# Sort's place stage held until the messages are done, the count stage's bank with its low digits outermost, and sort's operands loaded a group ahead

## The chip, the core and the metric

The kernel runs on one core of a Trainium2 chip. The metric is the device time of one execution in microseconds (us). Its engines are TensorE (PE, with its weight loads shown apart as PEld), VectorE (DVE), ScalarE (ACT), GpSimd (POOL) and SyncE (SP). In this kernel POOL does nothing but issue indirect DMAs (gathers and scatters by a list of rows, one for each 128 rows) after a few set-up instructions, and SP issues all other DMAs. Each engine runs its own instructions strictly in the order in which the program was built; semaphores tie the engines together.

## The reference, cut to what matters

Three branches are computed from the same normed nodes `xn` (3125 x 256) and added:

```python
def gnn(nodes, edges, senders, receivers, W_message, ...):
    msg_in = jnp.concatenate([nodes[senders], edges], axis=-1)         # 103125 x 320
    agg = jax.ops.segment_sum(msg_in @ W_message, receivers, 3125)
    h = layer_norm(relu(agg) + nodes, ...)
    return layer_norm(nodes + relu_mlp_skip(h, ...), ...)

def mix(x, ...):                                                       # 4 layers
    for i in range(4):
        x = x + linear_attn(layernorm(x), ...)                         # softmax over nodes for the keys
        x = x + gelu(layernorm(x) @ W1[i] + b1[i]) @ W2[i] + b2[i]

def ffn(x, ..., edge_index):                                           # 65536 edges, 4 experts
    h = x @ W_gat
    e = leaky_relu(a_src[src] + a_dst[dst]);  alpha = softmax of e over the edges of one dst
    agg = segment_sum(h[src] * alpha, dst);  w = top-2 gates of layernorm(agg)
    return sum over experts of gate * (gelu(x @ W1 + b1) @ W2 + b2)

xn = layernorm(x)
x = x + gnn(xn, ...) + mix(xn, ...)
x = x + ffn(layernorm(x), ...)
```

The `gnn` edges come sorted by receiver; the 65536 edges of `ffn` don't, so the kernel sorts them by `dst` itself.

## The kernel before, in words

Nodes lie in 25 tiles of 128 rows. Four kinds of work run side by side until about 1930 us; the last 520 us are the edges' softmax and the experts.

*Messages.* The 103125 edges are laid out as 128 partitions by 806 columns, so that each partition holds a run of edges in order of receiver. For each column, line 515 gathers one row of `xn` per partition (POOL), an SP load brings the edge features (line 494), and line 527 on DVE adds the column before it where the receiver stays the same. Columns come in chunks of 8 with three buffers (`m_run`); a finished chunk is stored to `run_d` (line 532). When all are summed, `message_nodes` closes the stage: `carries` (line 475) adds what crosses partitions, `fetch` gathers the sums of two node tiles at a time (line 595), and `pair` is the branch's MLP on them, a generator cut into `piece`s.

*The mixer.* Four layers over seven chunks of four tiles (`norm1`, `keys`, `context`, `combined`, `attend`, `ff_up`, `ff_down`), on PE, ACT and DVE. Line 1118 is the first product of each layer's `combined`.

*The sort* of the 65536 edges by `dst`, in 64 groups (`GROUPS`) of 8 columns of 128 edges (`GC`). A `dst` is split into a high digit (128 bins) and a low one (`LO` = 32). `count_group` makes one-hots of both digits on DVE (lines 695 and 701), multiplies them on PE (line 716) into a bank of PSUM laid out as column by low digit, evicts it on ACT into `cnts` (line 718), a 16-bit tile laid out as low digit by column, stores that to `counts_d` (line 719), and adds it to the table of all counts on PE one group later (line 723). `cnts` has two buffers. After the counts, `starts` makes the first place of each bin, `edge_ranges` the range of each node, and `ends_tile` (25 times) finds where each node's messages end. Then `place_group`, 64 times: SP loads the group's high digits as rows copied to all partitions (`hr`, 256 KB, line 756), DVE compares them with the partition's number (line 758) and makes the low one-hots again (`low_hots`, line 759), a scan (line 761) turns the stored counts into running ones, PE counts equal high digits among a column's edges (line 775), ACT turns that into "earlier" (line 776), and in the call after it PE and DVE look up each edge's place (lines 781 to 791). Every fourth call finishes 32 columns of `place`, and `clock["placed"]` says how many are ready. `send` (line 802) scatters one column of edges to its places (line 805, POOL).

*The edges' softmax and the experts.* Once all 512 columns are sent, `sorted_edges` loads the sorted list back and line 1294 gathers table rows by it (325 indirect DMAs), beside the expert MLPs on PE.

What sets the order is a planner that runs while the program is built. `clock["now"]` is a planned time; each step of the mixer calls `pace(us)`, which moves it on, runs one message `piece` if there is any, and adds every column that is due at `FIRST + COLUMN * (columns + 1)`, that is one per 1.27 planned us. When the last column is in, it sends up to 24 columns (`EARLY`), runs the jobs up to `ends_done`, and calls `message_nodes`; from then on columns are sent at the same spacing, as far as they are placed. The sort's steps stand in `jobs`; `beside(us)` runs as many as their planned costs allow (1.0 for a count group, 4.0 for a place group), but while messages are under way only as long as more than `held[0]` jobs are left. `held[0]` starts at `GROUPS - 12` and falls by 14 with each layer, so the place stage is spread over all four layers.

Of the kernel before, what the change touches and what calls it, by code (L numbers as in the profile page):

```python
# [8 lines left out]
F32 = mybir.dt.float32  # L9
BF16 = mybir.dt.bfloat16  # L10
I32 = mybir.dt.int32
F16 = mybir.dt.float16
# [6 lines left out]
P = 128  # L19
# [10 lines left out]
TM = -(-E // P)  # L30
# [5 lines left out]
DEPTH = 4  # L36
# [4 lines left out]
TE = E2 // P  # L41
NEXP = 4
GC = 8
GROUPS = TE // GC
SRC = 4096
LO = 32
# [13 lines left out]
def kernel(ctx: ExitStack, tc: tile.TileContext, a: dict, out: bass.AP):  # L60
    nc = tc.nc
# [174 lines left out]
    ps = pg.tile([P, DM], F32, name="ps_g")  # L236
# [171 lines left out]
        V.tensor_scalar(above, node_n, -1.0, SRC // 2 - 0.5, op0=ALU.mult, op1=ALU.add)  # L408

    def ends_tile(t):  # L410
        buf = so.tile([P, 8 * P], F16, name="ends_buf", tag="hr", bufs=2)
        at_least = buf[:, 6 * P:7 * P]
        V.tensor_scalar(at_least, row0, start_t[:, t:t + 1], None, op0=ALU.is_ge)
        T.matmul(first_ps[:, t:t + 1], at_least, ones_h, start=True, stop=True, skip_group_check=True)
        le, own = buf[:, :P], buf[:, P:2 * P]
        V.tensor_scalar(le, ids, whole_t[:, t:t + 1], None, op0=ALU.is_ge)
        T.matmul(whole_ps[:, t:t + 1], le, ones_h, start=True, stop=True, skip_group_check=True)
        V.scalar_tensor_tensor(own, ids, prev_t[:, t:t + 1], le, op0=ALU.is_ge, op1=ALU.subtract)
        for k, (c0, c1) in enumerate(((0, TM // 2), (TM // 2, TM))):
            ps = pa.tile([P, 512], F32, name="ps_a")  # L420
            T.matmul(ps[:, :c1 - c0], own, dst_h[:, c0:c1], start=True, stop=True)
            hit = buf[:, 2 * P:2 * P + TM // 2]
            S.activation(hit, ps[:, :c1 - c0], AF.Sign, bias=above[:, t:t + 1], accum_out=cnt2n[:, k, t:t + 1])
# [117 lines left out]


    FIRST, COLUMN, PIECE, EARLY = 52.0, 1.27, 0.9, 24
    clock = {"now": 45.0, "columns": 0, "sent": 0}

    pieces = []

# [4 lines left out]

    def pace(us):
        clock["now"] += us
        if pieces:
            piece()
        pinned = True
        while clock["columns"] < TM and FIRST + COLUMN * (clock["columns"] + 1) <= clock["now"]:
            sum_up(clock["columns"], pinned)
            pinned = False  # L560
            clock["columns"] += 1
            if clock["columns"] == TM:
                while clock["sent"] < min(EARLY, clock["placed"]):
                    send(clock["sent"])
                    clock["sent"] += 1
                for _ in range(len(jobs) - N_JOBS + ENDS):
                    jobs.pop(0)[1]()
                msgs.close()
                message_nodes()
        while (clock["columns"] == TM and clock["sent"] < clock["placed"]  # L570
               and FIRST + COLUMN * (TM + clock["sent"]) <= clock["now"]):
            send(clock["sent"])
            clock["sent"] += 1
# [125 lines left out]
    def low_hots(t):  # L699
        o = so.tile([P, GC, LO], F16, name="oh_lo", bufs=3)  # L700
        V.tensor_tensor(o, low_ids.rearrange("p (o l) -> p o l", o=1).to_broadcast([P, GC, LO]),
                        lo[:, t:t + GC].rearrange("p (t o) -> p t o", o=1).to_broadcast([P, GC, LO]), op=ALU.is_equal)
        return o

    counts_d = dram.tile([GROUPS, P, LO * (GC + 1)], F16, name="counts_d")
    counted = []
    cnts = [so.tile([P, LO, GC + 1], F16, name=f"counts{k}") for k in range(2)]
    for o in cnts:
        V.memset(o[:, :, 0], 0.0)

    def count_group(t):
        if t < TE:
            ohh, ohl = one_hot(t, hi, P, "oh_hi", 2), low_hots(t)
            ps = pg.tile([P, GC, LO], F32, name="ps_g")
            for i in range(GC):
                T.matmul(ps[:, i, :], ohh[:, :, i], ohl[:, i, :], start=i == 0, stop=i == GC - 1, skip_group_check=True)
            cnt = cnts[t // GC % 2]
            S.copy(cnt[:, :, 1:].rearrange("p l i -> p i l"), ps)  # L718
            nc.sync.dma_start(counts_d[t // GC, :, :], cnt.rearrange("p l i -> p (l i)"))
            counted.append((t, cnt))  # L720
        if t:
            t, cnt = counted.pop(0)
            T.matmul(table, ident_h, cnt.rearrange("p l i -> p (l i)"), start=t == 0, stop=t + GC == TE, skip_group_check=True)

    def split(x, near, rest):

        V.tensor_copy(near, x)
        V.tensor_tensor(rest[:, :, 0], x, near, op=ALU.subtract)
# [6 lines left out]
    def starts():  # L735
        cnt2 = so.tile([P, LO], F32, name="cnt2", tag="base")
        V.tensor_reduce(cnt2, table.rearrange("p (l i) -> p l i", i=GC + 1), AX.X, ALU.add)
        cum2 = so.tile([P, LO], F32, name="cum2", tag="oh_lo", bufs=3)
        V.tensor_tensor_scan(cum2, ones[:, :LO], cnt2, 0.0, op0=ALU.mult, op1=ALU.add)
        ps = pg.tile([P, LO], F32, name="ps_g")  # L740
        T.matmul(ps[:, :1], before, cum2[:, LO - 1:], start=True, stop=True)
        V.tensor_tensor(cum2, cum2, cnt2, op=ALU.subtract)
        base2 = so.tile([P, 1], F32, name="base2")
        V.tensor_copy(base2, ps[:, :1])
        V.tensor_scalar(cum2, cum2, base2, None, op0=ALU.add)
        nc.sync.dma_start(start_d, cum2)
        V.tensor_scalar(cum2, cum2, half, None, op0=ALU.add)
        places.append(parts(0))
        split(cum2, *places[0])

    def place_group(t):

        late = looks.pop() if looks else None
        if t < TE:
            hr = so.tile([P, GC, P], F16, name="hr", bufs=2)
            nc.sync.dma_start(hr.rearrange("p t e -> p (t e)"), row_h[t // GC:t // GC + 1, :].to_broadcast([P, P * GC]))
            ohT = ohTs[t // GC % 2]
            V.tensor_scalar(ohT[:P - 1], hr[:P - 1], bin_p[:P - 1], 2.0, op0=ALU.is_equal, op1=ALU.mult)
            ohl = low_hots(t)
            near, run_l = places.pop()  # L760
            V.tensor_tensor_scan(run_l.rearrange("p l i -> p (l i)"), goes.rearrange("p l i -> p (l i)"),
                                 run_l.rearrange("p l i -> p (l i)"), 0.0, op0=ALU.mult, op1=ALU.add)
# [15 lines left out]
        if late:  # L778
# [9 lines left out]
                    T.matmul(look[:, i, :], a1, a2, start=False, stop=k == 2, skip_group_check=True)  # L788
            own = so.tile([P, GC, LO], F32, name="own_bin", bufs=1)
            V.scalar_tensor_tensor(own, look, float(E2), ohl, op0=ALU.add, op1=ALU.mult)  # L790
            V.tensor_reduce(number[t // SG % 2][:, t % SG:t % SG + GC], own, AX.X, ALU.add)
            if (t + GC) % SG == 0:
                V.tensor_scalar_mul(number[t // SG % 2], number[t // SG % 2], 0.5)
# [2 lines left out]

    places = []
    looks = []
    SG = 4 * GC
    number = [so.tile([P, SG], F32, name=f"number{i}") for i in range(2)]  # L800

# [12 lines left out]
    ENDS = GROUPS + 1 + 2 + NT + 6  # L814
    jobs.insert(ENDS - 1, (1.0, ends_done))
    N_JOBS = len(jobs)
    held = [GROUPS - 12]
    spare_us = [0.0]

    def beside(us):  # L820
# [332 lines left out]
    def ff_down(l, c):  # L1153
        for i0, ts in enumerate(halves(c)):
# [9 lines left out]
            if l < DEPTH - 1:  # L1164
                for t in ts:
                    stats(xm[:, t, :], mv[:, t, :])
            beside(3.0 if 0 < l < DEPTH - 1 else 12.0)

    waiting = []
    gT = mx.tile([P, FF // P, 512], F32, name="gT")  # L1170
# [8 lines left out]
    for l in range(DEPTH):  # L1179
# [1 line left out]
        if l == 0:  # L1181
            fold(0)
        co = combined(kv, l)
        held[0] = GROUPS - 12 - 14 * l + 9 * (l > 0)
        beside(20.0)
        held[0] = GROUPS - 12 - 14 * l
        if l + 1 < DEPTH:
            att_w[l + 1] = layer_weights(l + 1)
        if l:
# [536 lines left out]
```

## Time and profile before

| | us |
|---|---|
| median of 3 runs (2451.12 to 2457.45) | 2451.38 |
| the profiled execution | 2454.66 |
| its span, first to last instruction | 2452.9 |

| where | from | to |
|---|---|---|
| layer 0 begins (line 1118) | 144 | |
| count groups on PE (line 716) | 145 | 335 |
| place groups on PE (line 775) | 500 | 1786 |
| layers 1, 2, 3 begin (line 1118) | 690, 1072, 1607 | |
| message gathers (line 515) | 34 | 1195 |
| scatters of sorted edges (line 805) | 1197 | 1908 |
| fetches of message sums (line 595) | 1232 | 1580 |
| row gathers of sorted edges (line 1294) | 1932 | 2349 |

The profile is of one execution. A group of instructions has one row: line, engine, operation, output and inputs, count, then busy time in us and the mean of one in ns, then how long the engine stood idle before such instructions and who ended that. "Issue" is time in which the engine waited for nothing that the profile shows. A row of waits reads: who waited, for whom, us in total, how often, and the longest.

### The profile page before, as it was taken

The numbers are of one execution on the slowest core, as the hardware profiler recorded it, in microseconds if no ns is written. First come the engines' busy times: TensorE is split into PE (matmuls) and PEld (weight loads), VectorE is DVE, ScalarE is ACT, GpSimd is POOL, SyncE is SP. The second block draws the span as 40 slices with busy tenths as digits, with TensorE's granted clock in tenths as the row PEclk, the third lists the DMA queues.
The fourth block names the chain that finished last, engine by engine and source line by source line (L and its number), as shares of the span: only waits on it lengthen the run. The fifth ranks groups of instructions, "written<-read, shape, count | busy, mean of one in ns | idle before, by whom it ended". The sixth has DMA issues, their size and how long they took to land. (4 is left out here: it accounts for less than half of the span.)

```text
span 2452.9 us, 32199 instructions
## 1 busy us (share of the span) xinstructions
PE 2048.4 (84%) x10075; PEld 1417.6 (58%) x10075; DVE 1510.4 (62%) x4536; ACT 1171.0 (48%) x2042; POOL 1720.3 (70%) x1740
## 2 busy tenths in 40 slices
PE   3869868686869998869589988989999889999976
PEld 2656645455546766646455666666767555556545
DVE  8886767758786776776534445466542355556536
ACT  5646565344444454445336656566544233333324
POOL 4666667757777777767767777777777777777742
PEclk9978878787889998979889999999999999999988
DMA  8986778878987888888611111222210112121101
GB/s 252 321 258 214 238 219 259 230 201 288 313 283 234 279 256 265 264 266 254 200 38 31 47 40 36 65 69 51 69 39 12 23 29 50 28 48 31 27 14 61
DMA packets 301773, 362.12 MB, mean 148 GB/s; under 512 B 183099, under 2 KB 248740, under 8 KB 288388
## 3 DMA queue, kind: packets, MB, share of 16 engines
q1 hardware_dynamic: 233076, 245.26, 31.6%
q0 software_dynamic: 68512, 114.67, 17.6%
q8 instruction: 82, 1.34, 0.2%
q14 instruction: 103, 0.84, 0.1%
HBM read 203.75 MB, written 160.11 MB: 148 GB/s over the span
## 5 line engine op out<-in xcount | busy, mean ns | idle before, releaser
L515 POOL DMA_INDIRECT m_run<-xn_d,src_i x806 | 814.2, 1010 | 376.3 <-issue 213.9
L805 POOL DMA_INDIRECT by_dst<-pairs,place x512 | 505.7, 988 | 156.1 <-issue 154.0
L527 DVE SCALAR_TENSOR_TENSOR m_run<-m_run,stay 128x320 f32<-128x320 f32 x805 | 439.2, 546 | 85.2 <-DMA m_run<-xn_d,src_i 72.3
L1149 PE MATMUL ps_a<-h,w 128*128 128x512 f32 (+1 forms) x896 | 387.7, 577 | 6.2 <-ACT h L165 6.1
L1294 POOL DMA_INDIRECT rows_c<-tab_d,si x325 | 319.1, 982 | 98.9 <-issue 97.1
L1160 PE MATMUL ps_a<-w,gT 128*128 128x256 f32 x1600 | 365.1, 383 | 0.0
L1160 PEld LDWEIGHTS ps_a<-w,gT 128*128 128x128 f32 x1600 | 303.1, 192 | 50.3 <-issue 7.6
L1149 PEld LDWEIGHTS ps_a<-h,w 128*128 128x128 f32 x896 | 164.7, 202 | 165.2 <-issue 146.0
L1150 ACT ACTIVATE gT<-ps_a,b 128x512 f32<-128x512 f32 (+1 forms) x224 | 140.8, 637 | 131.2 <-PE ps_a L1149 129.8
L124 ACT ACTIVATE hn<-xm,rstd 128x256 f32<-128x256 f32 x225 | 120.8, 594 | 60.3 <-DVE rstd L120 56.3
L776 ACT ACTIVATE earlier<-ps_t,slope 128x512 f16<-128x512 f32 x128 | 93.8, 772 | 115.0 <-PE ps_t L775 112.3
L160 PE MATMUL ps_t<-ident,hn 128*128 128x128 f32 x450 | 82.4, 313 | 48.5 <-ACT hn L124 41.8
L1415 ACT ACTIVATE hf<-ps_a,be 128x512 f32<-128x512 f32 (+1 forms) x112 | 70.3, 641 | 103.8 <-PE ps_a L1411 103.0
L1061 PE MATMUL ps_a<-wq,h 128*128 128x256 f32 x400 | 100.5, 394 | 20.0 <-ACT kT L1041 14.6
L1087 PE MATMUL ps_g<-xm,kr 128*128 128x256 f32 x400 | 108.1, 408 | 9.8 <-ACT kr L1085 9.5
L1029 PE MATMUL ps_a<-h,wk 128*128 128x512 f32 (+1 forms) x224 | 104.8, 604 | 2.7 <-ACT h L165 2.7
L1426 PE MATMUL ps_t<-we2h,hf 128*128 128x256 f32 x400 | 95.9, 392 | 10.8 <-ACT hf L1415 10.8
L160 PEld LDWEIGHTS ps_t<-ident,hn 128*128 128x128 f32 x450 | 56.0, 156 | 82.7 <-ACT hn L124 60.9
L1087 PEld LDWEIGHTS ps_g<-xm,kr 128*128 128x128 f32 x400 | 77.4, 202 | 42.0 <-ACT kr L1085 26.6
L718 ACT CAST counts<-ps_g 128x256 f16<-128x256 f32 x64 | 79.8, 1393 | 45.3 <-DMA counts_d<-counts 22.0
L1138 PE MATMUL ps_a<-co,hT 128*128 128x256 f32 x400 | 99.7, 392 | 0.8 <-DVE co L1129 0.6
L1061 PEld LDWEIGHTS ps_a<-wq,h 128*128 128x128 f32 x400 | 75.4, 195 | 40.8 <-ACT kT L1041 16.7
(441 smaller groups left out, 3812.4 us busy)
## 6 DMA issues: line engine op xcount, KB each, us to landing
run_d<-m_run SPq DMA_DIRECT2D x100, 1280.0 KB
m_run<-in_edge_attr_dram SPq DMA_DIRECT2D x95, 256.0 KB
hr<-row_h SPq DMA_DIRECT2D x64, 256.0 KB
m_run<-xn_d,src_i POOLq DMA_INDIRECT x806
w<-in_L_mix_W_dram SPq DMA_DIRECT2D x8, 1024.0 KB
by_dst<-pairs,place POOLq DMA_INDIRECT x512
rows_c<-tab_d,si POOLq DMA_INDIRECT x325
run_d<-rows_c SPq DMA_DIRECT2D x15, 312.0 KB
```

Of the source, the lines that this page charges most:

```text
L124: S.activation(dst, src, AF.Identity, bias=r[:, 1, i:i + 1], scale=r[:, 0, i:i + 1])
L160: T.transpose(ps[:, i * P:(i + 1) * P], src[:, c * P:(c + 1) * P], ident)
L515: last_gather[0] = G.indirect_dma_start(out=m[:, t, :D], out_offset=None, in_=xn_d, in_offset=bass.IndirectOffsetOnAxis(ap=src_i[:, t0 + t ...
L527: add = V.scalar_tensor_tensor(m[:, t, :], before_m, stay[:, c:c + 1], m[:, t, :], op0=ALU.mult, op1=ALU.add)
L805: i = G.indirect_dma_start(out=by_dst, out_offset=bass.IndirectOffsetOnAxis(ap=place[:, t:t + 1], axis=0), in_=pairs0[:, t:t + 1], in_offs ...
L1029: T.matmul(ps[:, :n], att_w[l]["wk"][:, kc, m * P:(m + 1) * P], h1[:, kc, :n], start=kc == 0, stop=kc == 1)
L1061: T.matmul(ps[:, i, :], h1[:, kc, o + i * P:o + (i + 1) * P], att_w[l]["wq"][:, kc, :], start=kc == 0, stop=kc == 1)
L1087: T.matmul(ps_x[:, m, :], kr[:, m * P:(m + 1) * P], xm[:, t, :], start=i == 0 and m == 0, stop=i == len(c) - 1, skip_group_check=True)
L1149: T.matmul(ps[:, :w], ff_w[l]["w1"][:, kc, f * P:(f + 1) * P], h2[:, kc, :w], start=kc == 0, stop=kc == 1)
L1150: S.activation(gT[:, f, :w], ps[:, :w], AF.Gelu, bias=ff_w[l]["b1"][:, f:f + 1])
L1160: T.matmul(ps[:, i, :], gT[:, f, (2 * i0 + i) * P:(2 * i0 + i + 1) * P], ff_w[l]["w2"][:, f, :], start=False, stop=f == FF // P - 1, skip_ ...
L1294: G.indirect_dma_start(out=rows_c[:, t - COLS[j], :], out_offset=None, in_=tab_d, in_offset=bass.IndirectOffsetOnAxis(ap=si[:, t:t + 1], a ...
```

## The change

- `held[0]` is `GROUPS - 5` throughout: until the last message column is summed the jobs stop with 59 left, which leaves six calls of `place_group` before it. After that `beside` gets 14 planned us, not 3, in the middle layers (and in the last one), once the messages are done.
- When the messages are done, pieces of the message MLP are held back for `COLUMN * (EARLY + 8)` = 41 planned us.
- The count stage's bank is laid out as low digit by column, so a product writes every eighth element of it and the eviction runs along both its sides. `cnts` gets four buffers (the two new ones share the tag of `run`), and a group is added to the table two groups later instead of one.
- The low one-hots of each count group are stored to DRAM (`lows_d`), and the place stage loads them instead of comparing again.
- `hr` and the low one-hots of a place group are loaded two calls ahead (`ahead_of`), the first two groups' in `starts`. `ends_buf` takes the tag `earlier` instead of `hr`.

```diff
--- before.py
+++ after.py
@@ -408,7 +408,7 @@
         V.tensor_scalar(above, node_n, -1.0, SRC // 2 - 0.5, op0=ALU.mult, op1=ALU.add)

     def ends_tile(t):
-        buf = so.tile([P, 8 * P], F16, name="ends_buf", tag="hr", bufs=2)
+        buf = so.tile([P, 8 * P], F16, name="ends_buf", tag="earlier", bufs=2)
         at_least = buf[:, 6 * P:7 * P]
         V.tensor_scalar(at_least, row0, start_t[:, t:t + 1], None, op0=ALU.is_ge)
         T.matmul(first_ps[:, t:t + 1], at_least, ones_h, start=True, stop=True, skip_group_check=True)
@@ -541,7 +541,7 @@


     FIRST, COLUMN, PIECE, EARLY = 52.0, 1.27, 0.9, 24
-    clock = {"now": 45.0, "columns": 0, "sent": 0}
+    clock = {"now": 45.0, "columns": 0, "fetched": 0.0, "sent": 0}

     pieces = []

@@ -552,7 +552,7 @@

     def pace(us):
         clock["now"] += us
-        if pieces:
+        if pieces and clock["now"] >= clock["fetched"]:
             piece()
         pinned = True
         while clock["columns"] < TM and FIRST + COLUMN * (clock["columns"] + 1) <= clock["now"]:
@@ -567,6 +567,7 @@
                     jobs.pop(0)[1]()
                 msgs.close()
                 message_nodes()
+                clock["fetched"] = clock["now"] + COLUMN * (EARLY + 8)
         while (clock["columns"] == TM and clock["sent"] < clock["placed"]
                and FIRST + COLUMN * (TM + clock["sent"]) <= clock["now"]):
             send(clock["sent"])
@@ -705,22 +706,25 @@
     counts_d = dram.tile([GROUPS, P, LO * (GC + 1)], F16, name="counts_d")
     counted = []
     cnts = [so.tile([P, LO, GC + 1], F16, name=f"counts{k}") for k in range(2)]
+    cnts += [so.tile([P, LO, GC + 1], F16, name=f"counts{k}", tag="run", bufs=2) for k in range(2, 4)]
+    lows_d = dram.tile([GROUPS, P, GC * LO], F16, name="lows_d")
     for o in cnts:
         V.memset(o[:, :, 0], 0.0)

     def count_group(t):
         if t < TE:
             ohh, ohl = one_hot(t, hi, P, "oh_hi", 2), low_hots(t)
-            ps = pg.tile([P, GC, LO], F32, name="ps_g")
+            ps = pg.tile([P, LO, GC], F32, name="ps_g")
             for i in range(GC):
-                T.matmul(ps[:, i, :], ohh[:, :, i], ohl[:, i, :], start=i == 0, stop=i == GC - 1, skip_group_check=True)
-            cnt = cnts[t // GC % 2]
-            S.copy(cnt[:, :, 1:].rearrange("p l i -> p i l"), ps)
+                T.matmul(ps[:, :, i], ohh[:, :, i], ohl[:, i, :], start=i == 0, stop=i == GC - 1, skip_group_check=True)
+            cnt = cnts[t // GC % 4]
+            S.copy(cnt[:, :, 1:], ps)
             nc.sync.dma_start(counts_d[t // GC, :, :], cnt.rearrange("p l i -> p (l i)"))
             counted.append((t, cnt))
-        if t:
-            t, cnt = counted.pop(0)
-            T.matmul(table, ident_h, cnt.rearrange("p l i -> p (l i)"), start=t == 0, stop=t + GC == TE, skip_group_check=True)
+            nc.sync.dma_start(lows_d[t // GC, :, :], ohl.rearrange("p t l -> p (t l)"))
+        while counted and (len(counted) > 2 or t >= TE):
+            now, cnt = counted.pop(0)
+            T.matmul(table, ident_h, cnt.rearrange("p l i -> p (l i)"), start=now == 0, stop=now + GC == TE, skip_group_check=True)

     def split(x, near, rest):

@@ -747,16 +751,23 @@
         V.tensor_scalar(cum2, cum2, half, None, op0=ALU.add)
         places.append(parts(0))
         split(cum2, *places[0])
+        for t in (0, GC):
+            ahead_of(t)
+
+    def ahead_of(t):
+        hr = so.tile([P, GC, P], F16, name="hr", bufs=2)
+        nc.sync.dma_start(hr.rearrange("p t e -> p (t e)"), row_h[t // GC:t // GC + 1, :].to_broadcast([P, P * GC]))
+        ohl = so.tile([P, GC, LO], F16, name="oh_lo", bufs=3)
+        nc.sync.dma_start(ohl.rearrange("p t l -> p (t l)"), lows_d[t // GC, :, :])
+        highs.append((hr, ohl))

     def place_group(t):

         late = looks.pop() if looks else None
         if t < TE:
-            hr = so.tile([P, GC, P], F16, name="hr", bufs=2)
-            nc.sync.dma_start(hr.rearrange("p t e -> p (t e)"), row_h[t // GC:t // GC + 1, :].to_broadcast([P, P * GC]))
+            hr, ohl = highs.pop(0)
             ohT = ohTs[t // GC % 2]
             V.tensor_scalar(ohT[:P - 1], hr[:P - 1], bin_p[:P - 1], 2.0, op0=ALU.is_equal, op1=ALU.mult)
-            ohl = low_hots(t)
             near, run_l = places.pop()
             V.tensor_tensor_scan(run_l.rearrange("p l i -> p (l i)"), goes.rearrange("p l i -> p (l i)"),
                                  run_l.rearrange("p l i -> p (l i)"), 0.0, op0=ALU.mult, op1=ALU.add)
@@ -788,6 +799,8 @@
                     T.matmul(look[:, i, :], a1, a2, start=False, stop=k == 2, skip_group_check=True)
             own = so.tile([P, GC, LO], F32, name="own_bin", bufs=1)
             V.scalar_tensor_tensor(own, look, float(E2), ohl, op0=ALU.add, op1=ALU.mult)
+            if t + 2 * GC < TE:
+                ahead_of(t + 2 * GC)
             V.tensor_reduce(number[t // SG % 2][:, t % SG:t % SG + GC], own, AX.X, ALU.add)
             if (t + GC) % SG == 0:
                 V.tensor_scalar_mul(number[t // SG % 2], number[t // SG % 2], 0.5)
@@ -796,6 +809,7 @@

     places = []
     looks = []
+    highs = []
     SG = 4 * GC
     number = [so.tile([P, SG], F32, name=f"number{i}") for i in range(2)]

@@ -814,7 +828,7 @@
     ENDS = GROUPS + 1 + 2 + NT + 6
     jobs.insert(ENDS - 1, (1.0, ends_done))
     N_JOBS = len(jobs)
-    held = [GROUPS - 12]
+    held = [GROUPS - 5]
     spare_us = [0.0]

     def beside(us):
@@ -1164,7 +1178,7 @@
             if l < DEPTH - 1:
                 for t in ts:
                     stats(xm[:, t, :], mv[:, t, :])
-            beside(3.0 if 0 < l < DEPTH - 1 else 12.0)
+            beside(12.0 if l == 0 else 14.0 if clock["columns"] == TM else 3.0)

     waiting = []
     gT = mx.tile([P, FF // P, 512], F32, name="gT")
@@ -1181,9 +1195,8 @@
         if l == 0:
             fold(0)
         co = combined(kv, l)
-        held[0] = GROUPS - 12 - 14 * l + 9 * (l > 0)
+        held[0] = GROUPS - 5
         beside(20.0)
-        held[0] = GROUPS - 12 - 14 * l
         if l + 1 < DEPTH:
             att_w[l + 1] = layer_weights(l + 1)
         if l:
```

## The prediction

> **What bounds the kernel now.** I read the page first, then the waits of POOL, then busy time by stage, then the waits inside the count stage. The page's chain of waits accounts for the last 80 us only, so it can't be used for the whole; the idle time of POOL can.
>
> ```profile
> span 2452.9 us, 32199 instructions
> PE 2048.4 (84%) x10075; PEld 1417.6 (58%) x10075; DVE 1510.4 (62%) x4536; ACT 1171.0 (48%) x2042; POOL 1720.3 (70%) x1740
> ...
> L515 POOL DMA_INDIRECT m_run<-xn_d,src_i x806 | 814.2, 1010 | 376.3 <-issue 213.9
> L805 POOL DMA_INDIRECT by_dst<-pairs,place x512 | 505.7, 988 | 156.1 <-issue 154.0
> ...
> L1294 POOL DMA_INDIRECT rows_c<-tab_d,si x325 | 319.1, 982 | 98.9 <-issue 97.1
> ```
>
> POOL is 70% busy, but each indirect DMA is followed by 0.3 us of issue, so a stretch with nothing else in it is full: one gather costs 1.010 + 0.30 = 1.31 us, one scatter 1.29. Its waits in the two stretches 34 to 1197 us and 1240 to 2350 us:
>
> ```profile
> POOL m_run L515 <- issue: 213.9, 702, 0.3
> POOL m_run L515 <- DVE m_run L527: 52.7, 21, 12.9
> POOL m_run L515 <- DVE digit L340: 29.2, 1, 29.2
> ```
>
> ```profile
> POOL by_dst L805 <- issue: 147.0, 482, 0.3
> POOL rows_c L1294 <- issue: 97.1, 319, 0.3
> ```
>
> In the second stretch nothing but issue and one wait of 3.8 us: POOL alone sets the pace from the end of the gathers to the end of the row gathers. In the first it also waits for column sums. So the span is a sum along POOL: the first gather starts at 33.8; 806 x 1.31 = 1056, one more gather 1.3, and what is left until the first scatter at 1196.7 is 105.6 us of waits; then 735.5 us to the first row gather at 1932.2 (563 indirect DMAs at 0.985 + 0.30 make 723 of it); then 520.7 to the end. The change can win in the 105.6, and lose there or by letting the scatters run dry.
>
> Busy time by stage (bounds are the layers' starts, by line 1118, and the last gather; columns: stretch, PE busy, PEld, DVE, ACT, POOL, clock, DMA share, GB/s):
>
> ```profile
> 144.00:340.00 196.00, 144.71 (x915) 106.25 (x916) 142.68 (x329) 117.77 (x130) 128.13 (x124) 0.79 0.72 231
> 340.00:500.00 160.00, 113.41 (x456) 73.31 (x454) 111.91 (x325) 72.56 (x172) 108.29 (x109) 0.84 0.81 227
> 500.00:690.00 190.00, 152.73 (x944) 111.30 (x944) 141.31 (x392) 91.86 (x163) 135.74 (x135) 0.85 0.87 276
> 690.00:1072.00 382.00, 332.55 (x1689) 234.68 (x1687) 273.61 (x714) 177.05 (x303) 281.70 (x281) 0.92 0.82 263
> 1072.00:1197.00 125.00, 106.39 (x631) 74.99 (x630) 98.52 (x270) 60.01 (x96) 86.26 (x87) 0.92 0.81 262
> 1197.00:1240.00 43.00, 10.65 (x57) 6.11 (x55) 5.06 (x13) 5.11 (x10) 30.52 (x32) 0.62 0.45 117
> 1240.00:1607.00 367.00, 333.22 (x1516) 233.79 (x1515) 171.34 (x516) 215.05 (x404) 277.56 (x283) 0.96 0.17 43
> 1607.00:1909.00 302.00, 287.07 (x1827) 207.21 (x1828) 154.67 (x551) 166.00 (x277) 231.10 (x233) 0.97 0.19 46
> ```
>
> Layer 0 (144 to 690) is where POOL is least full; in layer 1 (382 us for 281 gathers) it is full, 281.7 busy and about 84 of issue.
>
> **The change, part by part.** The built program's order, which holds no time, gives the columns summed when each layer starts: 63, 424, 703 before; 63, 402, 637 after. Place groups scanned on DVE before the last column: 37 before, 8 after. So 29 of 64 groups move behind the messages, and as the planner's clock no longer runs on for them, each layer carries fewer columns: layer 1 carries 235 instead of 279, and layer 2 holds 168 of them instead of 102. POOL's own order stays as it was but for where scatters and the 25 fetches alternate.
>
> Counts, in the waits of 144 to 340 us:
>
> ```profile
> PE sums_ps L723 <- ACT counts L718: 41.5, 43, 3.5
> ...
> DVE oh_hi L695 <- PE ps_g L716: 24.3, 31, 1.9
> ACT counts L718 <- DMA counts_d<-counts: 22.0, 14, 3.6
> ```
>
> PE stands at the table product until ACT has evicted the group, and DVE then waits for the one-hots that PE holds. Four banks and a product two groups later take away the 41.5 and the 22.0. The eviction, 1.39 us in its group's mean, becomes a contiguous write: between 0.47 (line 1085, 128x256 out of PSUM) and 0.66 (line 764, 128x256 in f16 from a strided read); by the latter 64 x 0.73 = 47 us of ACT, which hides behind PE and DVE. The strided PSUM write of line 716 has no row: its 512 products took 40.2 us busy, so between 0 and another 40 on PE; I take 0, since one product stays one product. Each group also writes its low one-hots to DRAM. They have three buffers, so DVE's compare waits for the write of three groups before: 3 x 3.03 us (64 groups in 194 us) = 9.1 us are there, and in the timeline the eviction ends 5 to 7 us after the compare and the second next eviction still waits until 2.6 to 5.3 us after a write was issued. With 0.7 us taken off the eviction and PE not blocked that is 7 to 11 us, so the new wait takes part of the gain. Of DVE's 24.3 I take 15; ends 0 and 24.3. DVE's two extra memsets are 0.085 us each, at the start.
>
> Operands ahead: before, the first two place groups start with
>
> ```profile
> L758 DVE TENSOR_SCALAR ohT<-hr,bin_p 127x1024 f16<-127x1024 f16 x2 | 1.0, 488 | 15.3 <-DMA hr<-row_h 15.3
> ```
>
> in 480 to 505 us, as the row copy can't be loaded while ends_tile holds the same buffers. With ends_buf in another tag both loads stand in starts(): 15.3 us off DVE, columns queued behind it included; ends 5 (the wait that follows there is for at_end_of) and 15.3. In later groups SP issues the load after the former use, so SP waits in order with weight and message loads behind it; it already waits so for line 756. 64 low compares (0.417 us) leave the place stage, and 128 DMAs of 64 KB come at 0.32 us of SP each (line 719): 41 us on a queue that mostly waits for stores to land.
>
> Now the sum. Layer 0: 546 - 22 columns x 1.31 - 15 - 15.3 = 487. Layer 1: POOL needs 235 x 1.31 = 308; PE's 332.6 less 26.5 for 14 place groups (lines 775, 788, 781 in that stage: 9.7, 12.7, 4.1) is 306, at the 95% of the stage 1607 to 1909 322. PE decides: 322. Layer 2 to its last column: POOL 168 x 1.31 = 220; PE 168 x 306/235 = 219, at 95% 230. The last gather then is at 144 + 487 + 322 + 230 = 1183 instead of 1197: 14 us sooner.
>
> Behind it POOL needs the same 735. Is it fed? PE busy there is 10.7 + 333.2 + 287.1 = 631; it gains 29 groups x 1.95 (124.8 us of the three lines over 64) = 57 and loses 219 - 90 = 129 that layer 2 has done already (90: 106.4 less 16 of place): 559, at 93% 601 us for 56 groups, 10.7 each, where POOL takes 8 x 1.285 plus 1.1 of fetches = 11.4. Covered, by 40 us; that cover is gone at a PE share of 87.6%, below it each per cent costs 7 us. The hold on message pieces (32 columns x 1.27 = 41 us) fills the 30.5 us in which PE waited at 1205 to 1236 for the first fetch; POOL sets this stage, so I cost it at nothing.
>
> One row speaks against the change: scatters took 72.14/75 = 0.96 us at 1300 to 1400 us, where 2 place groups ran, and 76.82/77 = 1.00 where 12 did. 29 x 8 x 0.04 = 9 us at most, given back by gathers that lose the same neighbours; I take 0. The Trainium skill, "SBUF — State Buffer", section "SBUF: two separate sides", has a harder rule: a two-port VectorE operation locks GpSimd out of descriptor writing, in its example 620 ns become 3100. By it one scatter for each moved group would cost 29 x 2.5 = 72 us; the row doesn't bear that out.
>
> So 2452.9 - 14 = 2439 by the profiled execution's span. That execution took 2454.7, the median is 2451.4; from the median **2437**.
>
> **Rivals.**
> *PE becomes the bound of the gather stage* (slower). PE has 306 + 219 = 525 busy in layers 1 and 2 up to the last column. For: it ran at 87% of layer 1. Against: POOL was full then, and DVE's 35.2 us of waits for landing gathers go when POOL is ahead; the stretch 1240 to 1430 us had 178/190 = 94%. At 87% the two take 603 instead of 552: +51 - 14 = +37, 2488. It costs more than it brings below 525/(1197 - 144 - 487) = 93%.
> *The gathers run at POOL's own pace.* 742 gathers from 144 us on at 1.31 = 972, and 20 of waits: last gather at 1136, 61 us sooner, 2390. For: DMA share 0.8 to 0.97 loses 29 row copies of 256 KB, and granted clock of 0.79 to 0.85 in layer 0 shows PE idle, not short. Against: 306 of 308 in layer 1.
> *The write of low one-hots takes the place of the removed wait.* Counts win nothing: +15, 2452; then nothing measurable changes.
>
> **How the numbers follow.** Forecast 0.40, PE bound 0.22, POOL's pace 0.24, the write 0.14. About 0.3% (7 us) is what a measurement here can tell from no change: 2444 to 2459. The forecast's own range is 2418 to 2456 (counts -9 to +15, the row copy up to +10, PE's share two points either way, 12, not all at once); it puts 0.30 of its 0.40 under it; POOL's pace adds 0.24, the write 0.02: faster 0.56. Same: 0.10 + 0.10 + 0.02 = 0.22. Slower: 0.20 + 0.02 = 0.22. The range reaches to most of both outer cases: 2392 to 2478.
>
> **What would show it.** The waits of line 723 for 718 gone, of 758 for hr gone; a new wait of the low compare for lows_d, about 9 us in all; the last line-515 gather near 1180; PE above 93% between layers 1 and 2; scatters behind nothing but issue, and 735 us from the first of them to the first row gather. I am wrong if that last stretch grows (place groups too late), or if layer 1 takes over 340 us for its 235 columns.

## The result and the profile after

The changed kernel takes 2463.93 us (median of 16 runs, 2456.26 to 2468.53) beside 2456.93 for the kernel before on the same chip (16 runs): ratio 1.0027, 95% interval 1.0016 to 1.0039. It is slower by about 7 us, where 14 less were forecast. The page of its profiled execution, span and engines first, then POOL's three large groups:

```profile
span 2457.2 us, 32417 instructions
...
PE 2039.7 (83%) x10075; PEld 1413.3 (58%) x10075; DVE 1502.4 (61%) x4474; ACT 1101.9 (45%) x2029; POOL 1724.5 (70%) x1740
...
L515 POOL DMA_INDIRECT m_run<-xn_d,src_i x806 | 815.0, 1011 | 380.6 <-issue 215.1
L819 POOL DMA_INDIRECT by_dst<-pairs,place x512 | 510.9, 998 | 156.1 <-issue 151.9
...
L1307 POOL DMA_INDIRECT rows_c<-tab_d,si x325 | 317.0, 975 | 98.9 <-issue 98.3
```

POOL's rows are those of before within 6 us, so next to nothing on POOL became dearer. The waits between the gathers add up to what they did (380.6 now, 376.3 before), though two of the waits that the change aims at (for the eviction in the count stage, and for the row copy) are nearly or wholly gone. POOL's waits from 1245 to 2357 us, from behind the first fetch to the end of the row gathers:

```profile
POOL by_dst L819 <- issue: 144.8, 475, 0.3
POOL rows_c L1307 <- issue: 98.3, 323, 0.3
POOL tgt_d L880 <- issue: 7.3, 24, 0.3
```

Hardly anything but issue is left, so this second stretch still has POOL's own length: 738.7 us from the first scatter (1201.8) to the first row gather (1940.5), 735.5 before. Whatever changed lies ahead of 1202 us. Busy time by stage there and behind it (stretch, PE, PEld, DVE, ACT, POOL, clock, DMA share, GB/s; layers 0, 1, 2 begin at 147, 645, 988, the last gather starts at 1200.6):

```profile
147.00:645.00 498.00, 396.07 (x2080) 275.26 (x2079) 363.15 (x941) 215.25 (x444) 356.73 (x344) 0.87 0.84 256
645.00:988.00 343.00, 310.65 (x1225) 213.48 (x1225) 219.35 (x534) 149.25 (x260) 235.53 (x239) 0.96 0.74 235
988.00:1201.00 213.00, 202.91 (x782) 136.28 (x783) 139.99 (x336) 95.59 (x158) 146.28 (x150) 0.98 0.75 241
```

```profile
1442.00:1820.00 378.00, 352.87 (x2556) 261.36 (x2556) 224.04 (x784) 232.40 (x408) 290.16 (x289) 0.96 0.28 72
1820.00:1940.00 120.00, 26.12 (x110) 18.81 (x109) 9.21 (x36) 9.59 (x17) 91.03 (x96) 0.60 0.03 4
```

Layer 0 is 48 us shorter than before, layer 1 39, and layer 2 up to the last gather 88 longer. In the last row PE works 26 of 120 us: the mixer ends early, and the kernel stands waiting for scatters. The change did free PE time, but where POOL sets the pace. In layer 1 POOL is busy 235.5 us; with 239 times 0.3 us of issue that makes 307 of 343 us, so it is no longer full. PE is at 90.6%.

POOL's longest waits from layer 1 to the last gather (645 to 1201 us) are, behind issue:

```profile
POOL m_run L515 <- DVE m_run L527: 23.0, 10, 6.7
POOL m_run L515 <- DVE rstd L120: 11.4, 2, 11.1
POOL m_run L515 <- DVE co L1143: 11.1, 1, 11.1
```

POOL waits for DVE, which has to finish a column's sum before the buffer is free for the next gather. What DVE waits for in the same stretch, first after, then before (690 to 1197 us):

```profile
DVE here L1044 <- PE ps_a L1043: 67.9, 20, 10.4
DVE xm L1153 <- PE ps_a L1152: 34.5, 4, 15.5
...
DVE m_run L527 <- DMA m_run<-xn_d,src_i: 13.6, 10, 2.7
```

```profile
DVE m_run L527 <- DMA m_run<-xn_d,src_i: 37.3, 25, 5.5
DVE here L1030 <- PE ps_a L1029: 33.5, 14, 7.6
DVE xm L1139 <- PE ps_a L1138: 12.2, 2, 6.4
```

Before, DVE waited 46 us for those two kinds of mixer product and 37 for gathers to land; after, 102 and 14. The sums now stand in DVE's order behind mixer instructions that wait for PE.

The count stage (first to last product: 147 to 323 us, 145 to 335 before), by groups and then by DVE's waits:

```profile
L719 PE MATMUL ps_g<-oh_lo,oh_hi 128*128 128x32 f16 x512 | 40.6, 228 | 14.2 <-DVE oh_lo L702 13.7 <-DVE cT L1136 0.3
...
L721 ACT CAST counts<-ps_g 128x256 f16<-128x256 f32 x64 | 23.6, 371 | 68.8 <-PE ps_g L719 54.1 <-issue 5.3 <-DMA lows_d<-oh_lo 4.5
...
L727 PE MATMUL sums_ps<-counts,ident_h 128*128 128x288 f16 x64 | 18.9, 309 | 5.2 <-ACT counts L721 5.2
```

```profile
DVE oh_hi L696 <- PE ps_g L719: 14.8, 18, 2.9
...
DVE oh_lo L702 <- DMA lows_d<-oh_lo: 6.1, 8, 2.8
```

PE's wait of 41.5 us at the table product is down to 5.2, and the eviction takes 0.37 us instead of 1.39. The new wait for the store of the low one-hots is there with 6.1 us, and DVE still waits 14.8 for the high one-hots.

At the start of the place stage, DVE's waits from 480 to 510 us after, and from 480 to 516 before:

```profile
DVE own_n L450 <- DMA own_n<-cnt_d: 16.1, 1, 16.1
DVE at_end_of L472 <- DMA at_end_of<-cnt_d,at_i: 6.1, 1, 6.1
```

```profile
DVE ohT L758 <- DMA hr<-row_h: 15.3, 2, 13.5
DVE at_end_of L472 <- DMA at_end_of<-cnt_d,at_i: 11.7, 1, 11.7
```

The 15.3 us for the row copy are gone, and DVE stands 16.1 us at line 450 instead, where it did not wait before. Line 446 stores the node counts, line 447 reads them back, and the store's round trip took 12.4 us on SP before and 15.2 after. Before, that time passed while DVE waited for the row copy. Of 27.0 us of waits 22.2 remain.

### The profile page after: what moved, and what is told of

The parts are those of the page before. It is cut to its first block, busy times and chain, and to the rows that moved or that the text cites. A ratio compares the mean times of both kernels' runs of the same rounds, so it can differ in the third digit from the quotient of the medians.

```text
span 2457.2 us, 32417 instructions
## 1 busy us (share of the span) xinstructions
PE 2039.7 (83%) x10075; PEld 1413.3 (58%) x10075; DVE 1502.4 (61%) x4474; ACT 1101.9 (45%) x2029; POOL 1724.5 (70%) x1740
## 5 line engine op out<-in xcount | busy, mean ns | idle before, releaser
L515 POOL DMA_INDIRECT m_run<-xn_d,src_i x806 | 815.0, 1011 | 380.6 <-issue 215.1
L819 POOL DMA_INDIRECT by_dst<-pairs,place x512 | 510.9, 998 | 156.1 <-issue 151.9
L1439 PE MATMUL ps_t<-we2h,hf 128*128 128x256 f32 x400 | 95.3, 390 | 8.1 <-ACT hf L1428 8.1
L110 DVE BATCH_NORM_STATS2 bst<-xm 128x6 f32<-128x256 f32 x250 | 97.2, 407 | 5.3 <-DVEq L303 3.6
L1439 PE MATMUL ps_t<-we,hf 128*128 128x256 f32 x400 | 95.0, 391 | 6.3 <-ACT hf L1428 6.3
```

The lines of the kernel that those rows point to most:

```text
L515: last_gather[0] = G.indirect_dma_start(out=m[:, t, :D], out_offset=None, in_=xn_d, in_offset=bass.IndirectOffsetOnAxis(ap=src_i[:, t0 + t ...
L819: i = G.indirect_dma_start(out=by_dst, out_offset=bass.IndirectOffsetOnAxis(ap=place[:, t:t + 1], axis=0), in_=pairs0[:, t:t + 1], in_offs ...
L1439: T.matmul(ps[:, i, :], hh[f][:, (i0 + i) * P:(i0 + i + 1) * P], we2[f], start=False, stop=f == FF2 // P - 1, skip_group_check=True)
```

## The experiments

Ratios are to the kernel before on the same chip, with 95% intervals; stage times come from each run's profiled execution.

**One part at a time.** The hold alone on the kernel before:

```diff
-        if pieces:
+        if pieces and clock["now"] >= clock["fetched"]:
...
-    held = [GROUPS - 12]
+    held = [GROUPS - 5]
...
-            beside(3.0 if 0 < l < DEPTH - 1 else 12.0)
+            beside(12.0 if l == 0 else 14.0 if clock["columns"] == TM else 3.0)
```

> The kernel before with the hold alone (held, the 14 planned us, the pause of the message pieces); counts and loads as before. Theory 1 (the hold thins the columns in layers 1 and 2, so PE sets their time there; POOL sets all the rest): last gather at about 147 + 517 + 343 + 213 = 1220 us against 1197 before, time 1.006 to 1.012 of before, PE done 60 to 110 us ahead of the first row gather. Theory 2 (the hold wins, and the new stores and loads of low one-hots give it back): last gather at 1160 to 1185, time 0.985 to 0.995.

2490.83 us, ratio 1.0117 (1.0096 to 1.0138): the hold costs some 29 us. The profiled execution took 2502.57, 12 above the median, so its stages show the loss somewhat too large. Its stages (layers 0, 1, and 2 to the last gather; columns as above):

```profile
147.00:677.00 530.00, 402.58 (x2078) 282.60 (x2076) 366.72 (x948) 268.97 (x443) 345.58 (x344) 0.83 0.78 234
677.00:1021.00 344.00, 310.00 (x1226) 212.78 (x1226) 220.24 (x535) 149.96 (x262) 235.39 (x239) 0.96 0.74 235
1021.00:1234.00 213.00, 203.11 (x783) 136.43 (x784) 140.19 (x336) 95.47 (x157) 148.05 (x150) 0.98 0.75 241
```

Layers 1 and 2 are those of the changed kernel to within a microsecond. They hold 239 and 150 gathers, where the kernel before has 281 and 86: 16 and 38 us are saved in layers 0 and 1, and 88 lost in layer 2. The hold is three edits, which no run takes apart; but up to the last column only the limit on the jobs can act, as the 14 planned us and the pause of the pieces come after it. Another 11 us are lost behind the messages (746.6 us from the first scatter to the first row gather, 735.5 before), 9.9 of them in one wait for places:

```profile
POOL by_dst L806 <- DVE place L688: 9.9, 1, 9.9
```

The changed kernel with its place groups spread as before (the same lines put back, with the two lines that lower `held[0]` by layer):

> The changed kernel with the place stage spread as before; bank, four buffers, low one-hots in DRAM and loads ahead kept. Theory 1: layer 0 loses 20 to 30 us, layers 1 and 2 carry their columns as before, last gather at 1165 to 1180, time 0.988 to 0.994 of before. Theory 2: last gather at 1197 to 1210, time 1.000 to 1.006.

2434.65 us, ratio 0.9901 (0.9881 to 0.9921), last gather at 1173.5. Against the changed kernel's 1.0027 the hold costs 1.3% in this company too. Its layer 0:

```profile
148.00:670.00 522.00, 408.18 (x2317) 286.13 (x2318) 390.47 (x1030) 229.86 (x465) 377.78 (x368) 0.86 0.85 265
```

That is 24 us less than before, and the hold takes it down by another 24, to 498.

The count stage alone: bank turned round, four buffers, table product two groups later.

```diff
+    cnts += [so.tile([P, LO, GC + 1], F16, name=f"counts{k}", tag="run", bufs=2) for k in range(2, 4)]
...
-                T.matmul(ps[:, i, :], ohh[:, :, i], ohl[:, i, :], ...)
+                T.matmul(ps[:, :, i], ohh[:, :, i], ohl[:, i, :], ...)
...
-            S.copy(cnt[:, :, 1:].rearrange("p l i -> p i l"), ps)
+            S.copy(cnt[:, :, 1:], ps)
```

> The kernel before with the count bank alone (low digit outermost, four buffers, product two groups later); no low one-hots in DRAM, no loads ahead. Theory 1: the count stage gets 10 to 20 us shorter, time 0.992 to 0.997. If the strided write into PSUM costs PE as much as the waits did: 0.999 to 1.003.

2430.79 us, ratio 0.9879 (0.9860 to 0.9899), better than expected. Its layer 0 is 25 us shorter than before, and its layers 1 and 2 (383 and 126 us) are within 1 us of it:

```profile
146.00:667.00 521.00, 406.53 (x2313) 287.19 (x2314) 393.12 (x1042) 229.62 (x464) 378.86 (x369) 0.83 0.84 258
```

The products now take 160 us from first to last (190 before, 175 in the changed kernel); DVE's wait at the high one-hots is

```profile
DVE oh_hi L695 <- PE ps_g L717: 4.0, 7, 0.9
```

instead of 24.3 before and 14.8 in the changed kernel. The part alone brings as much as all parts without the hold (0.9901), within the intervals.

The loads ahead and the stored low one-hots alone:

```diff
-        buf = so.tile([P, 8 * P], F16, name="ends_buf", tag="hr", bufs=2)
+        buf = so.tile([P, 8 * P], F16, name="ends_buf", tag="earlier", bufs=2)
...
+            nc.sync.dma_start(lows_d[t // GC, :, :], ohl.rearrange("p t l -> p (t l)"))
...
+        for t in (0, GC):
+            ahead_of(t)
```

> The kernel before with part three of the change alone: low one-hots written to DRAM and read back, row and low one-hots loaded two groups ahead, ends_buf in the earlier buffers. Theory 1, the removed waits of the place groups (15.3 us in layer 0) lie beside the gathers' own waits and come back as waits for the new loads: ratio 0.998 to 1.002, last gather within 6 us of 1196. Theory 2, the waits count as the prediction summed them (-15): last gather near 1181, ratio 0.994.

2460.15 us, ratio 1.0007 (0.9984 to 1.0029): no change that can be measured. The last gather is 10 us later, more than theory 1 allowed. Its DVE waits, in the count stage (two rows) and behind it (two rows):

```profile
DVE oh_hi L695 <- PE ps_g L717: 45.2, 38, 5.6
DVE oh_lo L701 <- DMA lows_d<-oh_lo: 7.8, 9, 2.0
```

```profile
DVE own_n L450 <- DMA own_n<-cnt_d: 15.5, 1, 15.5
DVE at_end_of L472 <- DMA at_end_of<-cnt_d,at_i: 6.1, 1, 6.1
```

The count stage is 14 us longer than before (204 against 190), as much as the same store takes from the count bank's gain (175 against 160). In return the place stage wins 27.0 - 21.6 = 5.4 us of waits.

**Why the hold costs.** The changed kernel with columns planned closer, so that more of them stand in layers 0 and 1:

```diff
-    FIRST, COLUMN, PIECE, EARLY = 52.0, 1.27, 0.9, 24
+    FIRST, COLUMN, PIECE, EARLY = 52.0, 1.15, 0.9, 24
```

> The changed kernel with one number changed: a column is planned every 1.15 us instead of 1.27, so layer 1 carries 260 columns instead of 235 and layer 2 94 instead of 162 by the plan. Theory 1: last gather near 1140 to 1160 instead of 1202, PE's slack ahead of the row gathers shrinks from 110 us to under 70, time 0.976 to 0.988 of before. Theory 2, and any theory in which DMA traffic or POOL already sets the gathers: last gather stays within 15 us of 1202, time 0.997 to 1.006.

2454.74 us, ratio 0.9982 (0.9967 to 0.9998), much less of a gain than theory 1 had. The last gather did come at 1159, 41 us sooner; but 774 us pass from the first scatter to the first row gather instead of 739. POOL's longest waits there, behind issue:

```profile
POOL aggr L596 <- PE ps_t L612: 21.0, 1, 21.0
POOL by_dst L819 <- DVE place L688: 13.6, 1, 13.6
```

This edit also plans the scatters closer. So the next run drew them apart, columns at 1.15 and scatters at 1.27 from the end of the messages:

```diff
-        while clock["columns"] < TM and FIRST + COLUMN * (clock["columns"] + 1) <= clock["now"]:
+        while clock["columns"] < TM and FIRST + MESSAGE * (clock["columns"] + 1) <= clock["now"]:
...
-               and FIRST + COLUMN * (TM + clock["sent"]) <= clock["now"]):
+               and clock["end"] + COLUMN * clock["sent"] <= clock["now"]):
```

> The changed kernel with the messages' columns planned 1.15 us apart instead of 1.27, and the scatters planned 1.27 us apart from the moment at which the messages end (in the run with COLUMN at 1.15 both were drawn together). By the plan layers 0 and 1 now hold 376 and 260 columns, near the 362 and 280 of before. Theory 1, the hold loses time because 66 columns were moved from beside place groups into layer 2, where PE is full, and the scatters of the 1.15 run starved because they were planned too close for the place groups: last gather near 1160, first row gather 739 us later, end near 2417, ratio 0.983. Theory 2, the place groups are late whenever they begin only after the messages: last gather near 1160, but 770 or more to the first row gather, ratio 0.996 to 1.000.

2444.54 us, ratio 0.9943 (0.9923 to 0.9964), between the two theories. In its profiled execution, which took 2431.27 and so lies 13 below the median, the last gather starts at 1154, and 755 us pass from the first scatter to the first row gather, of which

```profile
POOL by_dst L820 <- DVE place L689: 16.1, 2, 9.9
```

is the wait for places. So about two thirds of the hold's cost (1.0027 to 0.9943, of 1.0027 to 0.9901) come back when layers 0 and 1 get columns back by a closer plan. This kernel keeps its hold, its gathers end 20 us sooner than those of the kernel without hold, and it is still not faster than that one, as the scatters now wait for places. That the held place groups come late because they compete with the mixer for PE behind the messages is argued, not shown by a run of its own.

The same spacing on the count stage alone, whose place groups are spread:

> The kernel before with the count bank alone (0.988 of before), and the messages' columns planned 1.15 us apart with the scatters at 1.27 from the messages' end. Layers 0 and 1 now hold 400 and 309 columns by the plan, layer 2 only 21. Theory 1, a column costs more beside the mixer's layer 2 (1.47 us) than added to layers 0 and 1, whose POOL time per column is 1.31: last gather 1125 to 1160, ratio 0.970 to 0.984, and the best kernel so far. Theory 2, an added column costs as much in layers 0 and 1 as in layer 2, or the scatters starve: ratio 0.987 or more.

2493.58 us, ratio 1.0148 (1.0106 to 1.0189): theory 2, and far above the 0.987 at which it begins. The last gather is at 1139, 36 us sooner than at 1.27, and then the scatters stand still:

```profile
POOL by_dst L807 <- DVE place L688: 99.8, 2, 60.1
```

PE was busy 461.6 of 534 us from the last gather to layer 3 and 275.6 of 298 from there to the first row gather: the places came too late. A likely reason is that 806 columns in less time leave more of the mixer for later, with the place groups behind it; no run shows it apart.

Half of the second feed-forward product's steps left out in layers 1 to 3 of the changed kernel, to see whether PE sets layers 1 and 2:

```diff
+                fs = FF // P // 2 if l in (1, 2, 3) else FF // P
-                for f in range(FF // P):
+                for f in range(fs):
```

> The changed kernel with half of the products of the second feed-forward matrix left out in layers 1, 2 and 3 (200 of 400 products of 0.22 us in each), planned times as before. Theory 1, PE sets layers 1 and 2 while messages run, and POOL sets the time from the first scatter to the first row gather: last gather 35 to 60 us earlier (1141 to 1166), and still 739 us (within 8) from the first scatter to the first row gather, although layer 3 has 40 us less of products. Theory 2, gathers, DVE or transfers set layers 1 and 2: last gather 1190 or later.

One run of it took 2445.51 us, beside 2457.38 for the kernel before. Layers 1, and 2 to the last gather:

```profile
652.00:978.00 326.00, 277.03 (x1025) 180.57 (x1025) 214.78 (x533) 147.22 (x259) 237.32 (x239) 0.91 0.77 247
978.00:1187.00 209.00, 183.41 (x655) 114.98 (x656) 137.76 (x337) 96.42 (x158) 148.57 (x150) 0.94 0.77 246
```

The last gather comes at 1186, 15 us sooner: between theory 1's 35 to 60 and theory 2's 1190 or later. Layers 1 and 2 are 17 and 4 us shorter for 34 and 20 us less of PE time. POOL needs 500 us for their 389 gathers (383 busy and 0.30 of issue for each), so the two could have lost 56 of their 556. PE's products are thus part of the bound, not all of it: PE's wait for the mixer's own normed rows (line 160 for line 124) grew from 17 to 52 us. The other half of the expectation held: 735 us from the first scatter to the first row gather with less PE work in layer 3. So POOL sets that stretch.

**Looking for a better version.** The count stage alone with columns at 1.22, and the kernel without hold with columns at 1.20 and `beside` at 14 once the messages are done:

> The kernel before with the count bank alone, the messages' columns planned 1.22 us apart and the scatters 1.27 from the messages' end: between the count bank alone (columns at 1.27, ratio 0.988, scatters not starved) and the same at 1.15 (last gather 36 us earlier, but scatters starved for 100 us, ratio 1.015). Theory 1, the slack of the place groups and the mixer behind the scatters (some 20 us) takes up a shift of this size: last gather 1155 to 1165, end 10 to 15 us below the count bank alone, ratio 0.981 to 0.985. Theory 2, what the gathers gain the scatters give back at once: ratio 0.988 or more.

> The changed kernel without its hold (place groups spread over the message layers as before), columns planned 1.20 us apart, scatters 1.27 from the messages' end, and 14 planned us instead of 3 beside the mixer once the messages are done, so that place groups come sooner after them. Theory 1, scatters starved in the 1.15 runs because place groups came too late behind the mixer; with more of them beside each mixer step they keep ahead, and the earlier gathers pay: last gather 1145 to 1160, first row gather 732 to 742 us later, ratio 0.972 to 0.983. Theory 2, PE sets the time after the messages, whatever the order on it: the first row gather stays at 1905 or later, ratio 0.989 or more.

They took 3605.84 and 3705.71 us beside 3637.14 for the kernel before, which took 2456 to 2461 in every other group of runs: ratios 0.9928 (0.9898 to 0.9958) and 1.0192 (1.0150 to 1.0233), both what theory 2 had. As everything was so much slower there, they say little of the other runs, and the first was run again beside the count stage alone:

> The count bank alone with columns planned 1.22 us apart once more, because the chip of the last look granted a clock of 0.78 and ran the kernel before in 3637 us. Theory 1, slack behind the scatters takes up the shift: last gather 1155 to 1165, 10 to 15 us below the count bank alone of this call. Theory 2, what the gathers gain the scatters give back: within 5 us of the count bank alone, or above it.

> The count bank alone, columns at 1.27 as in the kernel before, on the same chip as the run beside it: ratio 0.986 to 0.990 on a chip that runs the kernel before in some 2457 us, last gather near 1176.

2436.38 us, ratio 0.9904 (0.9883 to 0.9924), which is theory 2, and 2427.44, ratio 0.9877 (0.9857 to 0.9897), as expected but for a last gather 10 us sooner. At 1.22 the gathers end 17 us sooner (1149 against 1166) and POOL gives it back:

```profile
POOL by_dst L807 <- DVE base L769: 28.9, 1, 28.9
```

The best kernel of the study is the count stage's part by itself, 1.2% below the kernel before in two runs and 1.5% below the changed one (0.9879 / 1.0027). The second kernel was not run again, so whether its order helps where the kernel before takes 2457 us stays open.

## Why the prediction was wrong

| step | predicted | measured |
|---|---|---|
| layer 0: columns moved out | -29 | -24 (498, against 522 without the hold) |
| layer 0: counts and loads ahead | -15 and -15.3 | -24 together (522, against 546) |
| layer 1 | -60 | -39 |
| layer 2 to the last gather | +105 | +88 |
| start of layer 0 | 0 | +3 |
| first scatter to first row gather | 0 | +3 |
| first row gather to the end | 0 | -4 |

The measured rows make up the 4.3 us between the two profiled spans, to about a microsecond; the medians lie 7 apart.

*The step that failed is layer 1*: "at the 95% of the stage 1607 to 1909 322. PE decides: 322." PE did decide more than before, but it was busy only 310.7 of 343 us, 90.6%. Of the 21 us by which 343 exceeds 322, 5 are work (310.7 against 306) and 16 the share. By parts of the layer (two rows after, then the end of layer 1 before):

```profile
645.00:885.00 240.00, 225.35 (x868) 154.09 (x868) 156.00 (x373) 101.18 (x169) 168.40 (x171) 0.96 0.74 237
885.00:988.00 103.00, 85.30 (x357) 59.38 (x357) 63.35 (x162) 48.08 (x93) 67.13 (x69) 0.93 0.73 230
970.00:1072.00 102.00, 84.65 (x362) 58.57 (x361) 67.48 (x174) 45.86 (x88) 72.94 (x75) 0.87 0.82 261
```

For 240 us PE is at 94%, in the last 103 at 83%; at 95% those 103 would have been 90, which is 13 of the 16 us. The end of layer 1 was at 83% before as well, and in both PE stands some 8 us at line 160 for the mixer's normed rows. There the last keys and context of the next layer are made. The stage from which the 95% were borrowed has none of them (no product of lines 1029, 1061 and 1087 before), as no layer follows the last; and layer 2's stretch to the last gather, which stops short of its layer's end, did run at 95.3%. That place groups beside the mixer are needed for 95% does not fit: layer 2's stretch had none. All this is read from the traces; no run changes the end of a layer alone.

So the rival in which PE becomes the bound is what came, at 91% and 95% in the two layers, where it had been priced at 87%. Its break-even share of 93% was about right, as both layers together make 513.6 / 556 = 92.4% and the last gather lies 5 us behind the time before.

*Mis-sized, too: the loads.* The lower end given, 5 us, is what came in waits (4.8), and alone the part brings no time at all (1.0007). The prediction named at_end_of as the wait that follows; it was own_n, a round trip through DRAM whose length the row copy's wait had hidden.

*Right in size, but by two errors that cancel:* counts. The forecast -15 holds for the length of the count stage as changed; alone the new bank gives -30 there (160 against 190), and with the store of the low one-hots 15 of it are lost. The prediction had a rival in which that store takes the whole gain, at 7 to 11 us of new waits. Here it took half of a gain of 30, and about as much in both pairs of runs that differ in the store (175 against 160, 204 against 190).

*Layer 2* was over-estimated (PE 203 us, not 219), which by luck hid part of the miss. *Behind the messages* the forecast held in the changed kernel: scatters behind issue alone. One of the two signs that it named for being wrong came true, layer 1 over 340 us for its columns. The rival with the gathers at POOL's own pace did not come. The scatters' row rose from 988 to 998 ns, 5.2 us over 512, inside the 9 allowed. The Trainium skill's lock between VectorE and GpSimd ("SBUF — State Buffer", section "SBUF: two separate sides") would, by an estimate from its example (620 ns become 3100), have cost 2.5 us for each place group moved. The row has 5.2 / 29 = 0.18 us for each.

What the prediction did not draw out of its own terms is that the hold is a loss: -29 - 60 + 105 = +16, carried by the two other parts. Run alone it costs 29 us by the medians. The mechanism is the planner's. A place group moves the planned clock by 4.0 us and so admits 3.15 columns, which need 3.15 x 1.29 = 4.1 us of POOL; on PE it costs 1.95. It is cheap company for gathers. The 21 groups that the planner no longer counts in layers 0 and 1 had let in 21 x 3.15 = 66 columns. In the run of the hold alone these two layers have 66 gathers fewer and are 54 us shorter, 0.8 us for each; layer 2 has 64 more and is 88 us longer, 1.4 for each. That the columns' place is what costs is borne out by the run with columns at 1.15 and scatters at 1.27, which brought two thirds back; the last third is not taken apart. PE's time saved behind the messages is worth nothing, as POOL needs its 735 us there in any case.

## What to carry to other kernels

Here moving work from a full stage to one with idle time on the same engine did not pay, as another engine set the time of the second stage and the moved work had let in what the bottleneck needs. Ask what each piece admits per microsecond of the scarce engine, not only what it takes. Where an order is planned by a clock, holding a job back also holds back everything that its planned time would have let in. A busy share used to turn work into time should come from a stage with the same steps in it, its end included, and a wait that is removed should be followed to the next one on the same engine: a store and its read-back may have been running behind it.

## What the hardware showed that was not expected

The eviction of a 128x256 bank to f16 fell from 1393 to 371 ns when source and destination run in the same order, 18 bytes apart before and contiguous after but for one gap in nine; less than either row by which it had been bounded (0.47 and 0.66). Products that write every eighth element of the bank cost little more: 228 ns against 215 in the mean, 190 against 176 for the shortest, 0.4 us busy over 512. PE's granted clock was higher, though, 0.90 in that stretch (147 to 323 us) against 0.79 before (145 to 336), so in clock periods the mean product is longer by up to a fifth, an estimate from these four numbers.

In one group of runs the kernel before took 3637 us instead of 2457. The record gives these runs the same chip number as four runs of this study in which it took 2457, so whether it was another chip is not shown. The page of the count stage's kernel with columns at 1.22 there:

```profile
L515 POOL DMA_INDIRECT m_run<-xn_d,src_i x806 | 807.4, 1002 | 721.4 <-issue 233.8
L807 POOL DMA_INDIRECT by_dst<-pairs,place x512 | 494.5, 966 | 350.3 <-issue 154.3
```

An indirect DMA takes as long as elsewhere (1023 and 987 ns in the same kernel when it took 2436 us), and the idle time before it has about doubled (320.1 and 187.8 there). PE's mean granted clock was 0.785, against 0.919. PE's busy time rose only from 2041.8 us to 2268.1, 226 of the 1168 us between the two profiled executions; what makes the rest was not found.
